# Turning the cross-attention weights on VectorE and regrouping them through DRAM, in a one-core decoder kernel

## The chip, the cores and the metric

The kernel runs on one core of a Trainium2 chip. The metric is the device time of one execution in microseconds (us). Before the change it was 3282.67 us, the median of three runs (3279.49, 3282.67 and 3287.01).

## What is computed

A post-norm decoder layer over 32 sequences of 256 tokens with 256 channels, all in float32. Three sub-layers follow each other, each added to its input and layer-normalised:

```python
# 1. latent self-attention: 16 heads, latent width 72, causal
Wdkv = x @ latent_w + latent_b
q = einsum('btc,hcl->bhtl', x, Wd_w) + Wd_b
attn = softmax(where(causal, q . Wdkv / 4, -inf));  y = attn . Wdkv;  x1 = norm(x + y @ out_w + out_b)
# 2. cross-attention to 120 context rows: 16 heads of width 64
q, k, v = x1 . Wq, ctx . Wk, ctx . Wv
weights = softmax(q k^T / 8);  x2 = norm(x1 + (weights . v) . Wo)
# 3. 16 experts, each of which takes its best 32 tokens of every sequence, and a shared expert
x3 = norm(x2 + routed(x2) + shared(x2))
```

The change concerns the middle sub-layer: `weights` come out of the softmax with the 256 queries on partitions (two tiles of 128) and the 120 keys along the row. The product `weights . v` contracts over the keys, so the weights must first be brought to a layout with the keys on partitions.

## The kernel before

One core does the sequences in **rounds**. In round n (`first_half(n)`, L939, then `second_half(n)`, L1008) TensorE works at three sequences at once: the self-attention of sequence n, the first half of the cross-attention (heads 0 to 7, called c0 = 0) of sequence n-1, and the rest of the cross-attention (heads 8 to 15, c0 = 4) of sequence n-2, with the norm and the store of sequence n-3. The rounds n = 1 to 30 and a first half for n = 31 run under a manual schedule of TensorE (PE), ScalarE (ACT), VectorE (DVE) and GpSimd (POOL): on these four the instructions stand in the order of the calls. The order on SyncE (SP), which issues the DMAs, is left to a scheduler. A tail of calls (`last_scores`, `last_weights`, and the end of the program) finishes the last sequences between the first pieces of the experts, which come after all rounds.

The self-attention of one sequence has four groups of heads. For group g: `queries(n, g)` makes the queries, `scores(n, g)` (L443) the scores, which DVE moves to `sm` while it adds a mask (L474); `peak` (L481) finds the negated maxima on DVE, `ex` (L488) takes exponentials on ACT with their sums, `over` (L497) inverts the sums on DVE and multiplies on POOL, and `turn` (L526) turns `sm` by 32x32 blocks with one DVE instruction (`nc.vector.transpose`, in the profile STREAM_TRANSPOSE, L533). `weigh(n, half)` (L549) multiplies the turned blocks by the values, and SP brings its result `z` to `zT` by DMA, in part through DRAM (`rest`, L581 to L587). `latent_out` (L592) multiplies `zT` by the output weights (36 matmuls), adds x (L602) and takes `moments` (L155): statistics on DVE and one power on POOL (L167). `norm_x1` (L605) normalises, `turn_x1` (L610) transposes x1 on TensorE (four transposes, `px1T`) and copies it to SBUF on DVE (L195). From this `x1T` come the cross queries `pqx` (L658).

The cross-attention of one sequence has four units, (c0, t) with c0 = 0 or 4 (eight heads each) and t = 0 or 1 (128 queries each). For each unit `cross_scores` (L677) makes two PSUM tiles of four heads ("even" and "odd" heads); `cross_peak`, `cross_ex` and `cross_over` do the softmax into a tile `xsm`, 128 queries by four heads by 120 keys, one for the even and one for the odd heads. Then `cross_turn` (L718) does, for each of the two tiles, four TensorE transposes into one PSUM bank and one copy to SBUF: DVE copies the even heads (L733), ACT the odd (L731). When both t of a half are there, `cross_weigh` (L735) multiplies `xpt` by the values. `cross_out` (L757) applies Wo, adds x1 (L767) and takes moments; `norm_x2` normalises, `store_x2` writes rows to DRAM, `turn_x2` transposes on TensorE (`px2T`).

The PSUM banks of all these share a ring of six (`r`); only `cross_scores` has banks of its own.

`keys(n+1)` (L363) makes the latent keys of the next sequence: four matmul instructions (`pk`), a copy with bias on ACT (`kT`, L372) and one on DVE (`kD`, L373). `place_keys` (L375) then sends parts of `kT` to the fixed tile `kr` with four small DMAs, one for each group of heads; each may go only when `scores` of the round before no longer needs that group.

In the order of the calls, `both(cross_turn, ...)` (L892: even, then odd) stands at four places of each round: after `ex(n, 0, 0)` in the first half (unit (0, 1) of sequence n-2), after `turn_x1` (unit (4, 0) of n-2), after `ex(n, 2, 0)` in the second half (unit (4, 1) of n-2) and after `ex(n, 3, 0)` (unit (0, 0) of n-1).

Of the kernel before, what the change touches and what calls it, by code (L numbers as in the profile page):

```python
# [20 lines left out]
F32 = mybir.dt.float32  # L21
# [5 lines left out]
P = 128  # L27
# [5 lines left out]
def decoder_kernel(  # L33
# [213 lines left out]

    vals = wp.tile([P, RB, TC, L], F32, name="vals")
    nc.gpsimd.memset(gw_sb, 0.0)

    raw = ow_sb.rearrange("p a b -> p (a b)").rearrange("p (c n) -> p c n", c=DC)
    by_head = raw.rearrange("p c (h l) -> p c h l", l=L)
# [339 lines left out]
    def latent_out(s):  # L592
        st = states[s]
        po = bank("r", [P, TC, C], f"po_{st['nm']}")
        for t in range(TC):
            project(
                po[:, t, :],
                [(st["zT"][:, c, t * P : (t + 1) * P], ow_sb[:, c, :]) for c in range(ZC)],
            )
        r1 = ap.tile([P, TC, C], F32, tag="r", bufs=1, name=f"r1_{st['nm']}")  # L600
        with urgent():
            nc.vector.tensor_tensor(r1, po, st["x"], ALU.add)  # L602
        st["r1"] = r1, *moments(ap, r1, f"1_{st['nm']}")

    def norm_x1(s):  # L605
        st = states[s]
        st["x1"] = ap.tile([P, TC, C], F32, tag="x1", name=f"x1_{st['nm']}")
        normalised(st["x1"], *st["r1"])

    def turn_x1(s):  # L610
        st = states[s]
# [46 lines left out]
    def cross_queries(s, c0, c):  # L658

        st = states[s]  # L660
        if c == 0:
            st["qxT", c0] = ap.tile([P, HG, T], F32, tag="qxT", name=f"qxT_{st['nm']}_{c0}")
        pqx = bank("r", [P, 2, T], f"pqx_{st['nm']}_{c0 + c}")
        for a in range(2):
            w0 = (c0 + c + a) * P
            project(
                pqx[:, a, :],
                [(wq_sb[:, d, w0 : w0 + P], st["x1T"][:, d, :]) for d in range(DC)],
            )
        dst = st["qxT", c0][:, c : c + 2, :]  # L670
        with urgent():
            if c:
                nc.vector.tensor_scalar(dst, pqx, XSCALE, None, ALU.mult)
            else:
                nc.scalar.mul(dst, pqx, XSCALE)

    def cross_scores(s, c0, t):  # L677
        st = states[s]
# [21 lines left out]
    def cross_ex(s, c0, t, odd):  # L700

        st = states[s]
        nm = f"x{st['nm']}_{c0}_{t}_{odd}"
        sm = ap.tile([P, HG, S2], F32, tag="xsm", bufs=4, name=f"xsm_{nm}")
        st["xrs", odd] = exponentials(sm, st["pL", c0, t][odd], st["xmax", odd], nm)
        st["xsm", c0, t, odd] = sm

    def cross_over(s, c0, t, odd):
        st = states[s]
        divide(st["xsm", c0, t, odd], st["xrs", odd])  # L710

    def cross_weights(s, c0, t):
        cross_peak(s, c0, t)
        for odd in range(2):
            cross_ex(s, c0, t, odd)
            cross_over(s, c0, t, odd)

    def cross_turn(s, c0, t, odd):  # L718
        st = states[s]
        nm = f"{st['nm']}_{c0}_{t}_{odd}"  # L720
        if t == 0:
            st["xpt", c0, odd] = ap.tile(
                [S2, HG, T], F32, tag=f"xpt{odd}", bufs=1, name=f"xpt_{nm}"
            )
        pT = bank("r", [S2, HG, P], f"pxT_{nm}")
        for j in range(HG):
            nc.tensor.transpose(pT[:, j, :], st["xsm", c0, t, odd][:, j, :], ident)  # L727
        dst = st["xpt", c0, odd][:, :, t * P : (t + 1) * P]
        with urgent():
            if odd:  # L730
                nc.scalar.copy(dst, pT)  # L731
            else:
                nc.vector.tensor_copy(dst, pT)  # L733

    def cross_weigh(s, c0):  # L735
        st = states[s]
        if c0 == 0:
            st["cxT"] = ap.tile([P, QC, T], F32, tag="cxT", bufs=1, name=f"cxT_{st['nm']}")
        for j0 in range(0, HG, 2):
            pc = bank("r", [P, 2, T], f"pc_{st['nm']}_{c0}_{j0}")  # L740
            for a in range(2):
                for odd in range(2):
                    nc.tensor.matmul(  # L743
                        pc[odd * DH : (odd + 1) * DH, a, :],
                        st["vx"][:, 2 * (c0 + j0 + a) + odd, :],
                        st["xpt", c0, odd][:, j0 + a, :],
                        start=True,
                        stop=True,
                    )
            dst = st["cxT"][:, c0 + j0 : c0 + j0 + 2, :]  # L750
            with urgent():
                if j0:
                    nc.scalar.copy(dst, pc)
                else:
                    nc.vector.tensor_copy(dst, pc)

    def cross_out(s):  # L757
        st = states[s]
        po2 = bank("r", [P, TC, C], f"po2_{st['nm']}")
        for t in range(TC):  # L760
            project(
                po2[:, t, :],
                [(st["cxT"][:, c, t * P : (t + 1) * P], wo_sb[:, c, :]) for c in range(QC)],
            )
# [3 lines left out]
        st["r2"] = r2, *moments(ap, r2, f"2_{st['nm']}")  # L768

    def norm_x2(s):  # L770
        st = states[s]
        st["x2"] = ap.tile([P, TC, C], F32, tag="x2", bufs=1, name=f"x2_{st['nm']}")
        normalised(st["x2"], *st["r2"])

    def store_x2(s):
        st = states[s]
# [162 lines left out]
    def first_half(n):  # L939
        odd = n % 2 and n > 1  # L940
        run(load, n + 1)
        scores(n, 0)
        run(cross_scores, n - 2, 4, 0)
        run(norm_x2, n - 3)
        run(store_x2, n - 3)
        run(cross_values, n - 1, 0)
        peak(n, 0)
        if n == 1:
            queries(1, 1)
        ex(n, 0, 0)  # L950
        both(cross_turn, n - 2, 0, 1)
        run(cross_peak, n - 2, 4, 0)
        if n != 1:
            queries(n, 1)
        over(n, 0, 0)
        if odd:
            run(cross_values, n - 1, 1)
        run(turn_x2, n - 3)
        ex(n, 0, 1)
        if odd:  # L960
            cross_keys(n // 2, 0, (0,))
        over(n, 0, 1)
        run(cross_ex, n - 2, 4, 0, 0)
        run(cross_over, n - 2, 4, 0, 0)
        weigh(n - 1, 1)
        place_values(n)
        if routed(n):
            route((n - 3) // BQ)
        turn(n, 0, 0)
        run(cross_weigh, n - 2, 0)  # L970
        run(cross_ex, n - 2, 4, 0, 1)
        run(cross_over, n - 2, 4, 0, 1)
        best_of(n, 0)

# [92 lines left out]
    def last_scores():  # L1067
# [1 line left out]
        scores(last, 2)  # L1069
        cross_scores(last - 1, 0, 0)  # L1070
        cross_queries(last - 1, 4, 0)
        both(cross_turn, last - 2, 4, 1)
        weights(last, 2)
        cross_queries(last - 1, 4, 2)
        cross_keys(last // 2, 1)
# [13 lines left out]
    def last_weights():  # L1089

        fill(1)
        turns(last, 3)
        finish_cross(last - 2)
        cross_scores(last - 1, 4, 0)
        both(cross_turn, last - 1, 0, 1)
        cross_weights(last - 1, 4, 0)
        fill(1)
        weigh(last, 1)
        cross_weigh(last - 1, 0)
        turn_x2(last - 2)  # L1100
        latent_out(last)
        norm_x1(last)

    def finish_cross(s):
        cross_out(s)
        norm_x2(s)
        store_x2(s)

# [327 lines left out]
```

## Time and profile before

| | |
|---|---|
| time of the profiled execution | 3281.89 us |
| its span, first to last instruction | 3280.1 us |
| granted TensorE clock, mean of the span | 0.997 |
| busy in the steady rounds (130 to 2150 us of the span): PE, DVE, ACT, POOL | 2004.42, 1343.54, 1105.96, 655.30 of 2020 us |
| share of the DMA engines there, and rate | 0.19, 46 GB/s |
| chain that ended last: PE, DVE | 91%, 5% of the span |
| cross transposes (`pxT`, L727): count, busy | 1024, 134.1 us |

The page of the profile sums each engine's busy time. Its groups give, for each line, engine and shape, the count, the busy time, the mean length of one instruction in ns, and the idle time before it with what ended it. The chain that ended last is followed back from the end, at each step to what released it; read in order of time, it says which engine set the pace at each moment. The timeline gives start and length of each instruction.

TensorE's instructions are pipelined: one can begin before the one before it has ended, so that a length is not the time by which an instruction moves the next. The starts of the next groups are.

### The profile page before, as it was taken

Reading aid. Unit: us, or ns where it says so; the run is one execution under the profiler, and the core shown is the slowest. Engines: PE = TensorE matmul, PEld = TensorE weight load, DVE = VectorE, ACT = ScalarE, POOL = GpSimd, SP = SyncE. Lnnn points to the kernel's source line nnn. Section 1 sums busy time; section 2 is a strip of 40 time slices with the busy share of each in tenths; the row PEclk is TensorE's granted clock in tenths of the full one; section 3 lists DMA queues with packets and bytes.
Section 4 is the critical chain, followed back from the end, with each engine's and each line's share of the span. In section 5 each row is a group of like instructions: output and inputs, shape, how many; then the busy total and the mean of one; then the engine's idle time right before and its main releaser. Section 6 shows DMA issues by size and latency. Waiting matters only on the chain.

```text
span 3280.1 us, 58501 instructions
## 1 busy us (share of the span) xinstructions
PE 3234.2 (99%) x21996; PEld 2375.4 (72%) x21996; DVE 1739.6 (53%) x3576; ACT 1391.5 (42%) x5237; POOL 1069.7 (33%) x951
## 2 busy tenths in 40 slices
PE   8999999999999999999999999999999999999999
PEld 6787778778777877877777878776556656655655
DVE  5666666666666666766666666653312233221133
ACT  4555555555555555555555555544211111111111
POOL 3323332333323323333333233332444302444400
PEclk9999999999999999999999999999999999999999
DMA  4121211111211112112121121133555522555421
GB/s 134 35 48 47 53 46 41 46 47 49 53 42 41 48 47 53 45 38 52 43 57 46 39 49 40 47 80 85 131 123 125 137 76 61 126 124 123 110 77 45
DMA packets 216610, 222.41 MB, mean 68 GB/s; under 512 B 37641, under 2 KB 192265, under 8 KB 216329
## 3 DMA queue, kind: packets, MB, share of 16 engines
q1 hardware_dynamic: 191536, 184.05, 21.0%
q0 software_dynamic: 24576, 34.62, 5.9%
q8 instruction: 175, 2.87, 0.4%
q14 instruction: 107, 0.87, 0.1%
q10 hardware_dynamic: 216, 0.01, 0.0%
HBM read 123.43 MB, written 57.41 MB: 55 GB/s over the span
## 4 chain that ended last, share of the span: by engine, by line
PE 91%; DVE 5%; POOL 1%; ACT 1%; DMA 1%; issue 1%; SPq 0%; POOLq 0%; ACTq 0%
PE po L201 13%; PE pz L559 8%; PE pqx L201 7%; PE pd L201 7%; PE pg L201 7%; PE pu L201 7%; PE pq L201 6%; PE pS L465 5%; PE pc L743 3%; PE pu_s L201 3%; PE pg_s L201 3%; PE pxT L727 3%; PE pfo L201 3%; PE pL L684 3%; PE pS L453 3%; PE pvx L201 3%
## 5 line engine op out<-in xcount | busy, mean ns | idle before, releaser
L499 POOL TENSOR_TENSOR sm<-sm,rs 128x512 f32<-128x512 f32 (+1 forms) x256 | 375.7, 1468 | 1126.1 <-DVE rs L498 1126.0
L488 ACT ACTIVATE sm<-sm,nmax 128x128 f32<-128x128 f32 (+1 forms) x1024 | 451.2, 444 | 105.3 <-DVE nmax L481 105.2
L488 ACT ACTIVATE xsm_x<-pL,nmax_x 128x120 f32<-128x120 f32 x1024 | 351.5, 364 | 3.5 <-DVE nmax_x L481 3.5
L499 POOL TENSOR_TENSOR xsm_x<-xsm_x,rs_x 128x480 f32<-128x480 f32 x256 | 252.7, 987 | 267.2 <-DVE rs_x L498 146.6
L1210 POOL DMA_INDIRECT acc<-eo,offs x128 | 200.8, 1569 | 335.9 <-DVE eo L1207 294.8
L201 PE MATMUL pq<-xT,wd_sb 128*128 128x256 f32 x1152 | 278.7, 382 | 0.3 <-DVE wd_sb L307 0.3
L559 PE MATMUL pz<-d,vals 32*72 32x256 f32 x4608 | 268.4, 380 | 3.7 <-DVE sm L474 1.8
L474 DVE TENSOR_TENSOR sm<-pS,mask 128x384 f32<-128x384 f32 x512 | 247.4, 543 | 36.0 <-PE pS L465 35.9
L201 PE MATMUL po<-ow_sb,zT 128*128 128x256 f32 x1152 | 260.9, 383 | 4.4 <-DMA zT<-z 4.4
L1281 DVE TENSOR_TENSOR hT<-gl,pu 128x512 f32<-128x512 f32 x128 | 87.9, 687 | 333.4 <-PE pu L201 254.2
L533 DVE STREAM_TRANSPOSE d<-sm 128x512 f32<-128x512 f32 (+1 forms) x256 | 244.9, 957 | 23.9 <-POOL sm L499 23.8
L201 PE MATMUL pg<-xeT,wg 128*128 128x512 f32 x512 | 242.3, 596 | 2.3 <-issue 2.3
L201 PEld LDWEIGHTS po<-ow_sb,zT 128*128 128x128 f32 x1152 | 214.3, 190 | 41.7 <-issue 10.0
L201 PE MATMUL pqx<-x1T,wq_sb 128*128 128x256 f32 x1024 | 242.1, 385 | 0.8 <-DVE x1T L195 0.8
L201 PE MATMUL pu<-xeT,wu 128*128 128x512 f32 x512 | 240.7, 592 | 0.0
L559 PEld LDWEIGHTS pz<-d,vals 32*72 32x72 f32 x4608 | 180.4, 139 | 81.9 <-issue 19.1
L481 DVE TENSOR_REDUCE nmax<-sm 128x4 f32<-128x512 f32 (+1 forms) x256 | 231.6, 946 | 3.3
L201 PEld LDWEIGHTS pq<-xT,wd_sb 128*128 128x128 f32 x1152 | 209.0, 190 | 28.1 <-DVE wd_sb L307 0.8
L201 PE MATMUL po<-wo_sb,cxT 128*128 128x256 f32 x1024 | 227.6, 380 | 0.0
L201 PE MATMUL pd<-wd,hT 128*128 128x256 f32 x1024 | 226.6, 379 | 0.0
L488 ACT ACTIVATION_READ_ACCUMULATOR xsm_x<-pL,nmax_x 128x1 f32 x1024 | 216.7, 212 | 0.0
L201 PEld LDWEIGHTS pd<-wd,hT 128*128 128x128 f32 x1024 | 192.1, 190 | 25.7 <-issue 1.0
(135 smaller groups left out, 5513.2 us busy)
## 6 DMA issues: line engine op xcount, KB each, us to landing
zT<-z SPq DMA_DIRECT2D x128, 256.0 KB
wg<-in_wg_dram SPq DMA_DIRECT2D x32, 512.0 KB
wu<-in_wu_dram SPq DMA_DIRECT2D x32, 512.0 KB
wd<-in_wd_dram SPq DMA_DIRECT2D x32, 512.0 KB
vals<-vd SPq DMA_DIRECT2D x128, 72.0 KB
x<-in_x_dram SPq DMA_DIRECT2D x32, 256.0 KB
rows<-x SPq DMA_DIRECT2D x32, 256.0 KB
acc<-x SPq DMA_DIRECT2D x32, 256.0 KB
```

Source lines behind the costliest of these rows:

```text
L201: nc.tensor.matmul(acc, lhsT, rhs, start=(i == 0), stop=(i == n - 1))
L453: nc.tensor.matmul(pS[j][:, SEG[t]], st["q8"][rows, t * P : (t + 1) * P], kr[rows, g, 0 : (t + 1) * P], start=(t == TC - 1), stop=False,)
L465: nc.tensor.matmul(pS[2 * a + odd][:, SEG[t]], st["qT", g][rows, a, t * P : (t + 1) * P], k[rows, 0 : (t + 1) * P], start=False, stop=(t = ...
L474: nc.vector.tensor_tensor(sm[:, j, :], pS[j], mask, ALU.add)
L481: nc.vector.tensor_reduce(nmax, src, AX.X, ALU.max, negate=True)
L488: nc.scalar.activation(dst[:, a, :], src[:, a, :], AF.Exp, bias=nmax[:, a : a + 1], accum_out=rs[:, a, :],)
L499: nc.gpsimd.tensor_tensor(dst, dst, rs.to_broadcast(list(dst.shape)), ALU.mult)
L533: nc.vector.transpose(st["d", t][:, :, k * HG : (k + 1) * HG, :].rearrange("p b h i -> p h b i"), st["sm", g][:, :, SEG[t]].rearrange("p h ...
L559: nc.tensor.matmul(pzs[r][:, t, :], vals[rows, at[0], at[1], :], st["d", t][rows, b].rearrange("p h i -> p (h i)"), start=(i == 0), stop=( ...
L684: nc.tensor.matmul(pLs[odd][:, j, :], st["qxT", c0][rows, j, t * P : (t + 1) * P], pairs[s // 2]["kxT", c0][rows, j, s % 2, :], start=True ...
L727: nc.tensor.transpose(pT[:, j, :], st["xsm", c0, t, odd][:, j, :], ident)
L1210: nc.gpsimd.indirect_dma_start(out=acc[b], out_offset=self.rows(b), in_=eo[:, k, :], in_offset=None, compute_op=ALU.add,)
```

## The change

In the rounds, the weights are no longer turned by TensorE. `cross_spread` turns each `xsm` by 32x32 blocks on DVE, into a tile `xb` that holds both the even and the odd heads. A block turn leaves the four groups of 32 keys side by side in the row and the four groups of 32 queries on partitions; it takes five DMAs from SP to exchange them: `xb` is written to DRAM (512 KB, 4 KB a partition), and four reads, one for each group of 32 keys, bring it back into `xpt` (128 KB each, in runs of 1 KB). `xsm` becomes four fixed tiles, widened to 128 keys, the last eight zero. `xpt` becomes one tile for even and odd heads in which a head's 256 queries lie in eight runs of 32; `cross_weigh` reads them so. `cross_turn` stays for the 16 tiles of the tail.

Beside that, calls move: each `cross_spread` stands later than the `cross_turn` that it takes the place of; the call of `keys(n+1)` moves from the second half to the place before `turn_x1` in the first; the moments are called on their own, those of x2 behind the mask additions of the next `scores`; `norm_x2`, `store_x2` and `turn_x2` stand later; `place_values` stands later; and ACT takes over the second `pqx` copy of each half from DVE.

```diff
+    xsms = [[cw.tile([P, HG, P], F32, name=f"xsm_{o}_{k}") for k in range(2)] for o in range(2)]
...
+            nc.gpsimd.memset(xsms[o][k][:, :, S2:], 0.0)
...
-        st["r1"] = r1, *moments(ap, r1, f"1_{st['nm']}")
+        st["r1"] = r1
+
+    def moments_x1(s):
+        st = states[s]
+        st["m1"] = moments(ap, st["r1"], f"1_{st['nm']}")
...
-            if c:
-                nc.vector.tensor_scalar(dst, pqx, XSCALE, None, ALU.mult)
-            else:
-                nc.scalar.mul(dst, pqx, XSCALE)
+            nc.scalar.mul(st["qxT", c0][:, c : c + 2, :], pqx, XSCALE)
...
+    def by_keys(s, c0, t):
+        st = states[s]
+        if ("xpt", c0) not in st:
+            st["xpt", c0] = ap.tile(
+                [P, TC * RB, 2 * HG, KB], F32, tag="xpt", bufs=1, name=f"xpt_{st['nm']}_{c0}"
+            )
+        return st["xpt", c0][:, t * RB : (t + 1) * RB, :, :]
...
+    def cross_spread(s, c0, t, odd):
+
+        st = states[s]
+        nm = f"{st['nm']}_{c0}_{t}"
+        if odd == 0:
+            st["xb"] = ap.tile([P, RB, 2 * HG, KB], F32, tag="xblk", bufs=1, name=f"xb_{nm}")
+        nc.vector.transpose(
+            st["xb"][:, :, odd * HG : (odd + 1) * HG, :].rearrange("p b h i -> p h b i"),
+            st["xsm", c0, t, odd].rearrange("p h (b i) -> p h b i", i=KB),
+        )
+        if odd == 0:
+            return
+        n = 2 * HG * KB
+        blocks_of = dram.tile([P, RB * n], F32, tag="xblk", bufs=4, name=f"xd_{nm}")
+        nc.sync.dma_start(out=blocks_of, in_=st["xb"].rearrange("p b h i -> p (b h i)"))
+        by_block = blocks_of.rearrange("(r i) (b n) -> b i r n", i=KB, b=RB)
+        dst = by_keys(s, c0, t).rearrange("p r h i -> p r (h i)")
+        for b in range(RB):
+            nc.sync.dma_start(out=dst[b * KB : (b + 1) * KB], in_=by_block[b])
...
-                        st["xpt", c0, odd][:, j0 + a, :],
+                        st["xpt", c0][0:S2, :, odd * HG + j0 + a, :],
...
-        run(norm_x2, n - 3)
-        run(store_x2, n - 3)
+        run(moments_x2, n - 3)
         run(cross_values, n - 1, 0)
         peak(n, 0)
...
+        run(norm_x2, n - 3)
+        run(store_x2, n - 3)
         ex(n, 0, 0)
-        both(cross_turn, n - 2, 0, 1)
...
-        run(turn_x2, n - 3)
         ex(n, 0, 1)
...
         over(n, 0, 1)
+        run(turn_x2, n - 3)
...
-        place_values(n)
...
         run(cross_scores, n - 2, 4, 1)
+        place_values(n)
...
         turn(n, 1, 0)
+        both(cross_spread, n - 2, 4, 0)
         run(cross_over, n - 2, 4, 1, 0)
         latent_out(n - 1)
+        moments_x1(n - 1)
...
         norm_x1(n - 1)
+        run(keys, n + 1)
         turn_x1(n - 1)
-        both(cross_turn, n - 2, 4, 0)
...
         cross_queries(n - 1, 0, 0)
+        both(cross_spread, n - 2, 4, 1)
         cross_queries(n - 1, 0, 2)
...
-        both(cross_turn, n - 2, 4, 1)
         cross_peak(n - 1, 0, 0)
...
-        run(keys, n + 1)
         ex(n, 3, 0)
-        both(cross_turn, n - 1, 0, 0)
         run(place_keys, n + 1)
+        both(cross_spread, n - 1, 0, 0)
         cross_peak(n - 1, 0, 1)
...
         cross_over(n - 1, 0, 1, 1)
+        both(cross_spread, n - 1, 0, 1)
         run(cross_out, n - 2)
```

More of the change, by code (lines that the diff above doesn't have):

```diff
@@ L249, in decoder_kernel @@
     nc.gpsimd.memset(gw_sb, 0.0)
+    xsms = [[cw.tile([P, HG, P], F32, name=f"xsm_{o}_{k}") for k in range(2)] for o in range(2)]
+    for o in range(2):
+        for k in range(2):
+            nc.gpsimd.memset(xsms[o][k][:, :, S2:], 0.0)
     raw = ow_sb.rearrange("p a b -> p (a b)").rearrange("p (c n) -> p c n", c=DC)
@@ L607, in norm_x1 @@
         st["x1"] = ap.tile([P, TC, C], F32, tag="x1", name=f"x1_{st['nm']}")
-        normalised(st["x1"], *st["r1"])
+        normalised(st["x1"], st["r1"], *st["m1"])
     def turn_x1(s):
@@ L669, in cross_queries @@
             )
-        dst = st["qxT", c0][:, c : c + 2, :]
         with urgent():
-            if c:
-                nc.vector.tensor_scalar(dst, pqx, XSCALE, None, ALU.mult)
-            else:
-                nc.scalar.mul(dst, pqx, XSCALE)
+            nc.scalar.mul(st["qxT", c0][:, c : c + 2, :], pqx, XSCALE)
     def cross_scores(s, c0, t):
@@ L703, in cross_ex @@
         nm = f"x{st['nm']}_{c0}_{t}_{odd}"
-        sm = ap.tile([P, HG, S2], F32, tag="xsm", bufs=4, name=f"xsm_{nm}")
-        st["xrs", odd] = exponentials(sm, st["pL", c0, t][odd], st["xmax", odd], nm)
+        sm = xsms[odd][t]
+        st["xrs", odd] = exponentials(sm[:, :, 0:S2], st["pL", c0, t][odd], st["xmax", odd], nm)
         st["xsm", c0, t, odd] = sm
@@ L709, in cross_over @@
         st = states[s]
-        divide(st["xsm", c0, t, odd], st["xrs", odd])
+        divide(st["xsm", c0, t, odd][:, :, 0:S2], st["xrs", odd])
     def cross_weights(s, c0, t):
@@ L720, in cross_turn @@
         nm = f"{st['nm']}_{c0}_{t}_{odd}"
[L721 to L724, printed above, removed]
+        dst = by_keys(s, c0, t)[0:S2, :, odd * HG : (odd + 1) * HG, :]
         pT = bank("r", [S2, HG, P], f"pxT_{nm}")
         for j in range(HG):
-            nc.tensor.transpose(pT[:, j, :], st["xsm", c0, t, odd][:, j, :], ident)
-        dst = st["xpt", c0, odd][:, :, t * P : (t + 1) * P]
+            nc.tensor.transpose(pT[:, j, :], st["xsm", c0, t, odd][:, j, 0:S2], ident)
+        src = pT.rearrange("p h (r i) -> p r h i", i=KB)
         with urgent():
             if odd:
-                nc.scalar.copy(dst, pT)
+                nc.scalar.copy(dst, src)
             else:
-                nc.vector.tensor_copy(dst, pT)
+                nc.vector.tensor_copy(dst, src)
+    def cross_spread(s, c0, t, odd):
[16 more added lines that the diff above has]
+            nc.sync.dma_start(out=dst[b * KB : (b + 1) * KB], in_=by_block[b])
     def cross_weigh(s, c0):
@@ L767, in cross_out, with moments_x2 @@
             nc.vector.tensor_tensor(r2, po2, st["x1"], ALU.add)
-        st["r2"] = r2, *moments(ap, r2, f"2_{st['nm']}")
+        st["r2"] = r2
+    def moments_x2(s):
+        st = states[s]
+        st["m2"] = moments(ap, st["r2"], f"2_{st['nm']}")
     def norm_x2(s):
@@ L772, in norm_x2 @@
         st["x2"] = ap.tile([P, TC, C], F32, tag="x2", bufs=1, name=f"x2_{st['nm']}")
-        normalised(st["x2"], *st["r2"])
+        normalised(st["x2"], st["r2"], *st["m2"])
     def store_x2(s):
@@ L1071, in last_scores @@
         cross_queries(last - 1, 4, 0)
-        both(cross_turn, last - 2, 4, 1)
         weights(last, 2)
@@ L1101, in last_weights @@
         latent_out(last)
+        moments_x1(last)
         norm_x1(last)
@@ L1105, in finish_cross @@
         cross_out(s)
+        moments_x2(s)
         norm_x2(s)
```

## The prediction, made before the changed kernel had run

> **What bounds the kernel now.** I read the page first (busy time), then the groups by shape, then the chain that ended last in order of time over two rounds (1080 to 1180 us), then the timeline where that chain leaves TensorE.
>
> The page's first line, and three groups (count, then busy us, mean ns of one, idle time before them):
>
> ```profile
> PE 3234.2 (99%) x21996; PEld 2375.4 (72%) x21996; DVE 1739.6 (53%) x3576; ACT 1391.5 (42%) x5237; POOL 1069.7 (33%) x951
> ...
> L727 PE MATMUL pxT<-ident,xsm_x 128*120 128x128 f32 x1024 | 134.1, 274 | 2.2 <-POOL xsm_x L499 2.2
> ...
> L733 DVE COPY xpt<-pxT 120x512 f32<-120x512 f32 x128 | 87.7, 685 | 5.2 <-PE pxT L727 1.3
> L533 DVE STREAM_TRANSPOSE d<-sm 128x512 f32<-128x512 f32 x128 | 87.7, 685 | 3.6 <-POOL sm L499 3.5
> ```
>
> TensorE is busy almost always; DVE has a third of each round free (1343.54 of 2020 us busy), ACT nearly half. So a microsecond taken from TensorE is a microsecond of the kernel until another engine's chain is late. The chain by time (start, us, what) shows what TensorE's pieces are worth and where it is near to waiting:
>
> ```profile
> 1105.67 0.70 DVE r L602
> 1106.39 0.75 DVE st L163 x2
> 1107.66 0.69 POOL rstd L167
> 1108.37 1.80 DVE x L173 x2
> 1110.22 0.55 PE px1T L191 x3
> 1110.77 0.87 PE pxT L727 x8
> 1111.64 3.63 PE pqx L201 x16
> ...
> 1135.90 0.86 PE pk L201 x4
> 1136.76 0.87 PE pxT L727 x8
> 1137.64 0.86 PE pq L201 x4
> ```
>
> Eight transposes (one call for even and odd) hold the chain for 0.87 us. The norm of x1 is on the chain itself, and the eight transposes behind `px1T` are what TensorE does while DVE copies `x1T`.
>
> **What goes.** Only 16 of the 256 tiles are still turned by `cross_turn`, so 960 transposes go: 120 calls of eight. By their starts this is 120 x 0.87 = **104.4 us**, 3.48 us in each of 30 rounds. (By the busy column it would be 960 x 134.1 / 1024 = 125.7 us. The Trainium skill, Perfetto Trace Analysis, Identifying the Most-Contended Engine, holds matmul busy time a bad measure because matmuls are pipelined; the trace agrees, 0.109 us from start to start against 0.131 busy; by the busy column the sum below would be 3183.)
>
> **What other engines gain or lose in a round.** DVE: eight block turns of the shape of L533, 8 x 0.685 = 5.48, less four copies L733 (2.74) and two `pqx` copies L673 (2 x 0.691): +1.4 us. ACT: less four copies L731 (4 x 0.572), plus two `pqx` copies (2 x 0.598): -1.1. POOL nothing. No engine becomes the bound by its sum; what counts is the order. The new right operand of `cross_weigh` and the copies into it lie in runs of 32; DVE's copy of `z`, into runs of 32 too, takes 681 ns for 512 columns against 685 for L733, so I cost this at nothing. TensorE's price for it no row shows: nothing, or at worst twice the present 1.88 us of a `pc` piece.
>
> **Wait 1: x1T.** The cover of the `x1T` copy goes, and `pk` stands before `px1T`. Two rows give the order of the copies of `pk`:
>
> ```profile
> 1136.80 0.47 ACT L372 ACTIVATE kT<-pk,latb 96x256 f32<-96x256 f32 x1
> ...
> 1137.30 0.48 DVE L373 TENSOR_SCALAR kD<-pk,latb 64x256 f32<-64x256 f32 x1 [1.03 <-ACT kT L372]
> ```
>
> ACT first, then DVE; and `kD` now stands on DVE before the copy of `x1T`. In the round of 1105 us: TensorE ends its other work at 1109.55, `pk` at 1110.41 (before the norm would hold it up no more), `kT` from 1110.61 to 1111.08, `kD` to 1111.59, `x1T` (0.69) to 1112.28, `pqx` 1112.33 instead of 1111.64: 0.7 us later though eight transposes are gone, and `pk` (0.86) is gone from the second half. Net -0.16 instead of -0.87: 0.7 lost. In the next round `pkx` ends at 1178.66, so `pk` at 1179.52, `kT` 1180.19, `kD` 1180.70, `x1T` 1181.39, `pqx` 1181.44 instead of 1180.96: net -0.38 instead of -0.87, 0.5 lost. Mean 0.6 x 30 = **18 us lost**. Behind `kD` on DVE wait `x1T`, a turn and the new block turns, all due later. `kT` earlier frees `place_keys` to go earlier; its four DMAs stand on SP among the new reads, each behind the `scores` that reads its part, and have the better part of a round.
>
> **Wait 2: x2T.** At the end of a round DVE has, in order: the last turn of `sm`, the last reciprocal, two block turns, the addition r2, four mask additions (1.94), the moments (1.17), two maxima (1.80), the norm of x2 (0.72). In the round that starts at 1063.68 with `scores(n, 3)`, call this 0: the last reciprocal was at 14.36 and comes 0.85 earlier, since ACT has lost `kT` and a copy ahead of it; 0.3 later POOL starts its product (0.99), and the second block turn (0.69) waits for that and ends at 15.6. Then 15.6 + 0.73 + 1.94 + 1.17 + 1.80 + 0.72 = 22.0 for x2. TensorE comes to `px2T` at 24.16 - 0.86 (`pk`) - 2 x 0.87 = 21.5. So in rounds of even n it waits some 0.6 us; in those of odd n it has 3.3 us more to do here (another `pvx`, `pkx`) and less before it, and doesn't wait. 15 x 0.6 = **9 us lost**. The moments moved behind the mask additions keep these from being later still.
>
> **The DMA trip.** The last block turn ends at 15.6; `cross_weigh` needs the data after `weigh`, at 26.7 (even) or 27.9 (odd). No row has this trip; near to it are SP's issues and the wait in the chain:
>
> ```profile
> 1163.28 0.27 SPq L581 DMA_DIRECT2D rest<-z  x1
> 1163.61 1.33 SPq L583 DMA_DIRECT2D zT<-z  x2
> ...
> 1166.08 0.49 SPq L587 DMA_DIRECT2D zT<-rest  x1
> ```
>
> ```profile
> 1163.61 0.65 SPq L583
> 1164.31 4.31 DMA zT<-z
> 1168.76 6.30 PE po L201 x28
> ```
>
> 64 KB had landed in DRAM 2.8 us after the start of their issue; two of 256 KB in runs of 1 KB 5.0 us after theirs. So the write of 512 KB takes 2.8 to 5.0. The reads are issued one after the other (0.66 each, as L398: 1.99 for three) and the last lands 2.8 to 5.0 after its issue: 2.0 + 2.8 to 2.0 + 5.0. Sum 7.6 to 12.0; I take 5.0 + 2.0 + 2.8 + 0.2 for SP = **10.0**, by `zT` for the write (same size) and by `rest` for the small last read. Landing at 25.6, 1.1 before it is due in even rounds and 2.3 in odd ones: nothing lost; with the upper end 0.9 x 15 = 14 us. The other group (c0 = 4) is due some 3 us later in its trip than this one. On SP the reads wait for their write and hold up what stands behind: for this group the stores of x2 and the loads of `vals`, which are not due before `weigh` ends, and then `rest`, `zT`, as before. `xb` has one buffer, so a block turn also waits for the write of the one before it, issued 7 us earlier. `xsm` is fixed now, so an exponential waits for a block turn of the same tile half a round before. `place_values` moves in the calls, but on SP its loads keep their places, three before `rest` and one after: nothing.
>
> **Sum.** 3281.9 (profiled execution; the median of the runs is 0.8 above) - 104.4 + 18 + 9 = **3205**.
>
> **Rivals.**
> (a) *The trip through DRAM is late.* Place: the first `cross_weigh` of each round; it waits T - 11.1 (even) or T - 12.3 (odd). For: five issues in line on one queue, a write that must land before the reads go, 0.2 of the DMA engines in use already. Against: the rows above, which end at 12.0. The forecast's gain of 77 us is 2.6 a round, so this decides from T = 14.3; at T = 16 it costs 4.3 x 30 = 129 us: 3334. (The Trainium skill, VectorE: DVE Perf Modes, The three transpose paths, warns that a plain DMA copy that transposes by strides is 19 times slower than the crossbar when the innermost destination stride is large, and its Rules for kernel authors leave a 128x128 transpose to TensorE. Here DVE has turned inside the blocks and the DMA moves runs of 1 KB; `zT<-z`, in runs of 1 KB, shows no such factor. By that rule the trip would be far beyond 14.3; beyond (a) I give it no chance of its own.)
> (b) *Nothing is late.* POOL and DVE run ahead of my sums, `kD` doesn't wait: 3281.9 - 104.4 = 3177.5. Against: the same order of `kT` and `kD` in both rounds looked at.
> (c) *DVE's chains are later than I sum them*, by up to a microsecond in each of the two waits and in odd rounds too, since the order is fixed and gaps between engines add up: 2 x 30 = 60 us more, 3265. For: DVE has 1.4 us more in a round that gets shorter. Against: a third of DVE's time is free.
> That the transposes stay on TensorE is excluded: the order of the changed program has 240 block turns for them.
>
> **Chances.** Forecast, within 20 us: 0.52. (b): 0.10. (c) and what lies between it and the forecast: 0.14. Within 0.2% (6.6 us, about what a measurement tells from no change): 0.05, a trip of some 14 us. Slower, by (a) or by a slow right operand (30 x 3.8 = 113 us): 0.19. So faster 0.76, same 0.05, slower 0.19. The range goes from (b) to a trip of about 14.5 us: 3178 to 3288; I leave out 0.05 below and 0.13 above.
>
> **What would show it.** Right: `pxT` L727 left with 64 instructions; idle time of `pqx` before DVE `x1T` near 18 us and of `px2T` before DVE x2 near 9; `pc` with no idle time before DMA `xpt`; steady rounds some 2.6 us shorter. Wrong: `pc` waiting for DMA (a), `pc` pieces longer than 1.88 us, or DVE's r2 and mask additions ending idle time on TensorE in odd rounds (c). The forecast fails if SP holds the last write back behind another wait.

## The result, and the profile after

The changed kernel takes **3211.17 us** (median of four runs, 3210.65 to 3212.54), against 3284.84 us for the kernel before on the same chip (four runs, 3279.49 to 3288.32): a ratio of 0.978, with an interval of 0.976 to 0.980. Its profiled execution took 3211.46 us with a span of 3209.7 us and a mean granted clock of 0.997, as before. That is 70.4 us less than the profiled execution of before (3281.89 us), 2.3 us in each of 30 rounds.

The page of the changed kernel begins with the busy times:

```profile
PE 3129.1 (97%) x21036; PEld 2276.3 (71%) x21036; DVE 1754.4 (55%) x3632; ACT 1360.9 (42%) x5181; POOL 1071.3 (33%) x955
```

TensorE's busy time fell by 3234.2 - 3129.1 = 105.1 us. Its idle time (span less busy) rose from 3280.1 - 3234.2 = 45.9 to 3209.7 - 3129.1 = 80.6 us, by 34.7. 105.1 - 34.7 = 70.4, the whole difference: by this split 105 us of work went, and a third of it came back as waiting. The split is not sharp, as the waits below show. DVE has gained 14.8 us, ACT has lost 30.6.

The groups by shape of the same kernel (count, busy us, mean ns, idle time before them and its releasers):

```profile
L201 PE MATMUL pqx<-x1T,wq_sb 128*128 128x256 f32 x1024 | 237.8, 385 | 38.0 <-DVE x1T L195 38.0
...
L753 DVE STREAM_TRANSPOSE xb<-xsm 128x512 f32<-128x512 f32 x240 | 156.3, 680 | 17.0 <-POOL xsm L504 17.0
L775 PE MATMUL pc<-xpt,vx 120*64 120x256 f32 x1024 | 124.6, 385 | 0.0
...
L739 PE MATMUL pxT<-ident,xsm 128*120 128x128 f32 x64 | 9.0, 278 | 2.4 <-POOL xsm L504 2.4
```

64 transposes are left; the 240 block turns cost 680 ns each; and `pc`, whose right operand now lies in runs of 32, has no idle time before it at all. The new idle time stands in front of `pqx`. TensorE's waits (in all us, how often, longest), of before and then of after:

```profile
PE px1T L191 <- DVE x L173: 13.2, 45, 0.6
PE po L201 <- DMA zT<-z: 4.4, 8, 1.6
```

```profile
PE pqx L201 <- DVE x1T L195: 38.0, 31, 1.4
PE po L201 <- DMA zT<-z: 6.7, 12, 1.6
PE px2T L191 <- DVE x L173: 4.6, 3, 1.5
...
PE px1T L191 <- DVE x L173: 1.3, 3, 0.6
```

The wait for x1 moved, from `px1T` to `pqx`, and grew: +37.2 (`pqx` waited 0.8 before) and -11.9 make 25.3 us of the 34.7. Part of a wait can also count as busy time. The groups of `px1T`, before and then after, have the same 128 transposes:

```profile
L191 PE MATMUL px1T<-ident,x 128*128 128x128 f32 x128 | 27.0, 295 | 14.2 <-DVE x L173 13.2
```

```profile
L191 PE MATMUL px1T<-ident,x 128*128 128x128 f32 x128 | 20.7, 280 | 1.4 <-DVE x L173 1.3
```

Before, the first transpose of a round ran ahead and the other three waited for the second half of x1: in the round of 1105 us they started 0.64 us after it (1109.58 and 1110.22), of which the list has 0.34 as idle. So 6.3 us of the 105.1 are this wait, and with them the net loss at x1 is 19.0 us rather than 25.3. The chain that ended last, in order of time (start, us, what), shows one such place:

```profile
1012.56 0.88 PE pk L201 x4
...
1013.46 0.48 ACT kT L377
...
1013.97 0.48 DVE kD L378
...
1014.48 0.70 DVE x1T L195
...
1015.22 3.72 PE pqx L201 x16
```

From the end of `pk` to `pqx` three copies follow one another for 1.78 us. Of these TensorE covers 0.5 with `px1T`; 1.23 us a time is idle (38.0 / 31).

The trip through DRAM, on the timeline of the round of 1049 us (DVE's last block turn, SP's write, SP's four reads, and the product that needs them):

```profile
1049.79 0.71 DVE L753 STREAM_TRANSPOSE xb<-xsm 128x512 f32<-128x512 f32 x1 [0.57 <-POOL xsm L504]
1050.53 0.34 SPq L761 DMA_DIRECT2D xd<-xb  x1
1053.13 1.73 SPq L765 DMA_DIRECT2D xpt<-xd  x4
...
1061.60 1.95 PE L775 MATMUL pc<-xpt,vx 120*64 120x256 f32 x16
```

and the table by stretches over it (us, PE busy, PEld, DVE, ACT, POOL, granted clock, share of the DMA engines, GB/s):

```profile
1054.90:1056.30 1.40, 1.40 (x8) 1.25 (x7) 1.40 (x3) 1.22 (x5) 0.54 (x1) 1.00 0.78 251
1056.30:1057.50 1.20, 1.14 (x7) 0.52 (x5) 1.20 (x5) 1.20 (x8) 0.00 (x0) 1.00 0.04 10
```

The reads go 2.6 us after the write, and by 1056.3 or soon after the DMA engines are idle: the trip lasts some 5.9 us from the end of the block turn (1050.50). It is due 11.1 us after it (1061.60). In the next round block turn and product are 12.4 us apart (1115.48 and 1127.88).

### The profile page after: what moved, and what is told of

Its sections match the earlier page's. It is cut to its first block, busy times and chain, and to the rows that moved or that the text cites. A ratio compares the mean times of both kernels' runs of the same rounds, so it can differ in the third digit from the quotient of the medians.

```text
span 3209.7 us, 57226 instructions
## 1 busy us (share of the span) xinstructions
PE 3129.1 (97%) x21036; PEld 2276.3 (71%) x21036; DVE 1754.4 (55%) x3632; ACT 1360.9 (42%) x5181; POOL 1071.3 (33%) x955
## 4 chain that ended last, share of the span: by engine, by line
PE 86%; DVE 5%; DMA 3%; ACT 3%; issue 1%; POOL 1%; SPq 1%; POOLq 0%; ACTq 0%; DVEq 0%
PE po L201 11%; PE pz L564 8%; PE pqx L201 7%; PE pd L201 7%; PE pu L201 7%; PE pg L201 7%; PE pq L201 7%; PE pS L470 5%; PE pu_s L201 3%; PE pg_s L201 3%; PE pfo L201 3%; PE pc L775 3%; PE pvx L201 3%; PE pL L689 3%; PE pkx L201 3%; PE pS L458 3%
## 5 line engine op out<-in xcount | busy, mean ns | idle before, releaser
L493 ACT ACTIVATE xsm<-pL,nmax_x 128x120 f32<-128x120 f32 x1024 | 351.7, 365 | 2.2 <-DVE nmax_x L486 2.2
L504 POOL TENSOR_TENSOR xsm<-xsm,rs_x 128x480 f32<-128x480 f32 x256 | 252.7, 988 | 240.9 <-DVE rs_x L503 239.9
L201 PEld LDWEIGHTS po<-ow_sb,zT 128*128 128x128 f32 x1152 | 214.3, 190 | 44.5 <-issue 12.4
L201 PEld LDWEIGHTS pq<-xT,wd_sb 128*128 128x128 f32 x1152 | 214.1, 190 | 43.7 <-issue 11.1
L201 PEld LDWEIGHTS pqx<-x1T,wq_sb 128*128 128x128 f32 x1024 | 189.4, 190 | 72.6 <-DVE x1T L195 45.4
L167 POOL TENSOR_TENSOR rstd<-rstd,mhalf 128x2 f32<-128x2 f32 (+1 forms) x97 | 67.3, 693 | 507.3 <-DVE rstd L166 455.7
```

The costliest lines, as they stand in the source:

```text
L201: nc.tensor.matmul(acc, lhsT, rhs, start=(i == 0), stop=(i == n - 1))
L493: nc.scalar.activation(dst[:, a, :], src[:, a, :], AF.Exp, bias=nmax[:, a : a + 1], accum_out=rs[:, a, :],)
L504: nc.gpsimd.tensor_tensor(dst, dst, rs.to_broadcast(list(dst.shape)), ALU.mult)
```

## The experiments

Theory: the 35 us that came back are the copies `kT`, `kD`, `x1T` in line before `pqx` (25), x2 a little late, and `zT`; the DMA trip costs nothing, since it is hidden with 5 us to spare. Rivals: the moved calls themselves do harm or good apart from that line; the loss is the extra DMA traffic; or the trip is nearer to its due time than it looks. In the table, idle is TensorE's span less its busy time.

| kernel | median us | ratio to before, interval | idle us |
|---|---|---|---|
| the change | 3211.17 | 0.978, 0.976 to 0.980 | 80.6 |
| keys_behind_turn | 3196.87 | 0.974, 0.972 to 0.975 | 60.9 |
| kD_behind_x1T | 3193.95 | 0.973, 0.972 to 0.974 | 66.0 |
| keys_as_before | 3219.16 | 0.981, 0.979 to 0.982 | 79.3 |
| moves_alone | 3280.69 | 0.999, 0.998 to 1.000 | 53.6 |
| block_turns_alone | 3212.71 | 0.978, 0.977 to 0.980 | 73.9 |
| one_more_hop | 3232.60 | 0.984, 0.983 to 0.986 | 103.4 |
| two_more_hops | 3622.84 | 1.103, 1.100 to 1.106 | 366.5 |
| two_hops_first_half_only | 3425.72 | 1.043, 1.040 to 1.046 | 236.3 |
| cover_q8 | 3181.52 | 0.968, 0.967 to 0.969 | 49.5 |
| cover_q8_early_x2 | 3177.26 | 0.967, 0.966 to 0.969 | 47.9 |

**kD behind the copy of x1T.**

```diff
-            nc.vector.tensor_scalar(st["kD"][LM:], pk[0:LM], latb[0:LM], None, ALU.add)
+        st["pk"] = pk
...
+    def keys_odd(s):
+        st = states[s]
+        with urgent():
+            nc.vector.tensor_scalar(st["kD"][LM:], st.pop("pk")[0:LM], latb[0:LM], None, ALU.add)
...
         turn_x1(n - 1)
+        run(keys_odd, n + 1)
```

> The changed kernel with only the DVE copy kD moved behind the copy of x1T; pk stays ahead of px1T on TensorE and kT stays on ACT. Theory (kD, waiting for kT, holds the x1T copy): the copy starts some 0.55 us sooner, 16 us in all: 3195; idle time of pqx before x1T falls from 38.0 to about 21, since nothing covers the copy itself (0.69 us). Rival (the copy waits for px1T or the norm, not for kD): no change, 3211.

It took 3193.95 us, 17 less than the change. Its waits and its chain:

```profile
PE pqx L201 <- DVE x1T L195: 22.8, 31, 0.8
```

```profile
1069.10 0.45 PE px1T L191 x4
1069.57 0.70 DVE x1T L195
1070.32 3.72 PE pqx L201 x16
```

`kD` (0.48 us and its step) is out of the line, and the wait fell by 15.2 us, 0.49 each time. What is left is the copy of `x1T` itself, 0.74 us from the end of `px1T` to `pqx`, which the eight transposes covered before.

**keys behind turn_x1.** `pk` itself then stands between `px1T` and `pqx`, as the eight transposes did.

```diff
-        run(keys, n + 1)
         turn_x1(n - 1)
+        run(keys, n + 1)
```

> The changed kernel with keys(n+1) called just behind turn_x1 instead of just ahead of it, so that TensorE's four pk instructions (0.86 us) stand between px1T and pqx, and kD stands behind the x1T copy on DVE. Theory (TensorE sets the pace and loses its time at the x1T copy, which waits for kT on ACT and kD on DVE): pk covers the copy as the transposes did, pqx comes 0.69 us sooner in even and 0.48 in odd rounds, about 18 us in all: 3193; idle time of pqx before DVE x1T falls from 38.0 to under 8, that of px1T before the norm rises from 1.3 to about 13. Rival (the wait only moves to the norm of x1, whose chain of DVE and POOL sets the pace here): no change, 3211.

It took 3196.87 us. Its waits:

```profile
PE px1T L191 <- DVE x L173: 14.8, 45, 0.8
PE po L201 <- DMA zT<-z: 9.5, 12, 1.9
PE px2T L191 <- DVE x L173: 4.6, 3, 1.5
```

The wait of `pqx` is down to the 0.8 us of before, and that of `px1T` is back. Two ways of breaking the same line gain 14 and 17 us: the line `kT`, `kD`, `x1T` is shown to cost that much.

**keys as before.** The call goes back to the second half, between `peak(n, 3)` and `ex(n, 3, 0)`.

> The changed kernel with keys(n+1) back in the second half, ahead of ex(n, 3, 0), where it stood before the change. Theory: nothing stands between px1T and pqx, but x1T no longer waits for kD, while px1T waits for the norm again; 0.1 us slower in even, 0.4 in odd rounds: 3218, within 3212 to 3226. Rival (that place of the keys is what keeps the gain of the eight transposes there): 0.86 us a round slower, 3237.

It took 3219.16 us, 8 more than the change:

```profile
PE pqx L201 <- DVE x1T L195: 22.8, 31, 0.8
PE px1T L191 <- DVE x L173: 13.1, 45, 0.6
```

Both waits stand side by side now, 35.9 us against 39.3 in the change. By the list alone it would be 3 us faster; but busy time is 9.0 us longer (3138.1 against 3129.1), 6.3 of it in `px1T`, which is split by its wait again (27.0 us against 20.7). So moving `keys` is a little better than leaving it, but it is its place against `turn_x1` that counts: one line further down it is worth 22 us, not 8.

**The moves alone, and the block turns alone.** In the first, `cross_turn` stays at its four places and all moved calls stay moved. The second is the kernel before with `cross_spread` at the places of the change, and no other call moved.

```diff
-        both(cross_spread, n - 2, 4, 0)
...
+        both(cross_turn, n - 2, 4, 0)
```

> The changed kernel with its weights turned by TensorE again: cross_turn at its four old places, no block turns and no DMAs for them; all the moved calls (keys, moments, norm_x2, store_x2, turn_x2, place_values, the pqx copy on ACT) stay. Theory (the gain is TensorE's time for 960 transposes; the moves only decide what is waited for): near the kernel before, 0.2 to 0.4 us a round off for pk as a cover: 3276, within 3268 to 3284. Rival (a good part of the gain comes from the moves, through DVE, which loses two copies a half): 3260 or below.

> The kernel before with the block turns and their DMAs at the places where the change has them, and with none of the other moves: keys, moments, norm_x2, store_x2, turn_x2, place_values and the pqx copies as before. Theory: the gain stays but for the x1T copy, which nothing covers now and which then also waits for the norm: near the version with the keys as before, 3214, within 3206 to 3224; idle time of px2T gone, since x2 no longer waits behind the mask additions and maxima. Rival (the moves are needed, since DVE's chain at the end of a round with moments ahead of the mask additions stops TensorE): 3240 or above.

The moves alone took 3280.69 us (ten runs) against 3284.07 (15 runs): 3 us. The block turns alone took 3212.71, the same as the whole change. Their waits, first of the moves, then of the block turns:

```profile
PE pqx L201 <- DVE x1T L195: 15.8, 30, 1.4
```

```profile
PE pqx L201 <- DVE x1T L195: 22.8, 31, 0.8
PE px1T L191 <- DVE x L173: 14.6, 45, 0.8
PE po L201 <- DMA zT<-z: 4.0, 7, 1.6
```

Even with the eight transposes as a cover, `kD` in the line makes `pqx` wait 15.8 us. Neither kernel has a wait of `px2T` for x2 in the list: the 4.6 us of the change need the block turns and the moved moments and norm together. The moves take away the wait of `px1T` and add as much elsewhere; the gain of the change is that of the block turns. These two runs also price the transposes like for like: with the moves on both sides TensorE's busy time fell by 3229.3 - 3129.1 = 100.2 us, without them by 3234.2 - 3136.2 = 98.0. And the wait of `po` for `zT`, 4.4 us before and 6.7 in the change, is 8.4 with the moves and none of the new DMAs, and 4.0 with the new DMAs and no moves.

**One more hop.** Each block is copied once more inside DRAM before it is read.

```diff
         nc.sync.dma_start(out=blocks_of, in_=st["xb"].rearrange("p b h i -> p (b h i)"))
+        for hop in range(1):
+            again = dram.tile([P, RB * n], F32, tag=f"xhop{hop}", bufs=4, name=f"xh{hop}_{nm}")
+            nc.sync.dma_start(out=again, in_=blocks_of)
+            blocks_of = again
```

> The changed kernel with one more copy of each 512 KB block from DRAM to DRAM between the write and the four reads, so that the trip gets about 2.8 us longer; the output is the same. Theory (the trip takes some 6 us of 11 to 13, by the trace of the changed kernel, and is hidden): at most a few us slower, 3211 to 3220. Rival (the trip is what TensorE's first cross_weigh of a round comes near to waiting for): 2.8 us x 30 = 84 us slower, 3295.

It took 3232.6 us, 21 more than the change: outside what either side had said. The timeline of an even round, whose last block turn ended at 1063.85 (write, hop, reads, product):

```profile
1063.88 0.36 SPq L761 DMA_DIRECT2D xd<-xb  x1
1067.22 0.49 SPq L764 DMA_DIRECT2D xh<-xd  x1
...
1070.96 1.78 SPq L769 DMA_DIRECT2D xpt<-xh  x4
...
1076.49 1.95 PE L779 MATMUL pc<-xpt,vx 120*64 120x256 f32 x16 [1.46 <-ACT z L582]
```

The product starts 12.6 us after the block turn and has waited 1.46, so it was due at 11.2. (The releaser named is not the real one, as can be when several semaphores are waited for: in the change the product at 1061.60 starts before ACT's copies of z, at 1061.73, so it does not need them.) The next, odd round does not wait. Over the whole run:

```profile
L779 PE MATMUL pc<-xpt,vx 120*64 120x256 f32 x1024 | 127.4, 391 | 24.4 <-DMA acc<-x 7.8 <-DMA xpt<-xh 7.1 <-DMA vals<-vd 5.5
```

The waits are uneven: 11 even rounds have 16.4 us of them (one alone 5.5), 5 odd ones 5.5 (one alone 3.2), and one product of heads 8 to 15 has 1.7. Most products don't wait at all. So the trip is near its due time with one hop, and how late it comes varies from round to round; what was wrong in the expectation was the length of the hop. The copy itself took 3.7 us; the write before it 3.3 instead of 2.6, and the reads after it were slower to land too (5.5 from the first issue to the product, where 3.3 were enough in the change): 6.7 in all in this round where I had put 2.8.

**Two more hops.** `range(2)` in place of `range(1)`.

> The changed kernel with two more copies of each 512 KB block from DRAM to DRAM between its write and its reads. From the run with one more hop: the trip was 5.9 us without a hop and about 12.4 us with one, and there an even round lost what went beyond 11.1 us, an odd round nothing up to 12.4. A second copy of about 3.7 us makes the trip about 16 us. If the price of a late trip is its length past 11.1 us in an even and past 12.3 us in an odd round, TensorE loses 4.9 and 3.7 us, 4.3 us on average over 30 rounds, about 129 us over the changed kernel: about 3340 us (3310 to 3360), and the wait of the cross product pc for DMA grows from about 20 to 110 to 130 us, now in nearly every round, odd ones too. Rival: what the one hop cost was not lateness of the trip but the displaced issues on the sync engine's queue, a fixed sum for each hop: then a second hop adds another 21 us, about 3254 us, with pc's wait near 40 us.

It took 3622.84 us, 283 above the forecast and far beyond the rival. The group of `pc`:

```profile
L779 PE MATMUL pc<-xpt,vx 120*64 120x256 f32 x1024 | 219.4, 602 | 292.6 <-DMA xpt<-xh 254.8 <-DMA rest<-z 32.2 <-DMA zT<-z 5.6
```

Against the change, idle time rose by 366.5 - 80.6 = 286 us and busy time by 3255.1 - 3129.1 = 126 us. Two things had been left out. First, there are 59 waits, not 30: the product of heads 8 to 15 was late too. Its last write stands on SP behind the reads of the trip before, and goes some 3 us after its block turn (at 1125.71, the turn ended at 1122.81; the product followed at 1141.32, 18.5 us after the turn; in the round before 3.25 us). Second, a `pc` matmul took 602 ns on the mean instead of 385. The timeline shows when (the last bracket is the wait):

```profile
1062.09 1.95 PE L779 MATMUL pc<-xpt,vx 120*64 120x256 f32 x16 [2.88 <-DMA xpt<-xh]
...
1079.43 0.33 SPq L761 DMA_DIRECT2D xd<-xb  x1
...
1082.68 0.47 SPq L764 DMA_DIRECT2D xh<-xd  x1
...
1087.26 1.67 SPq L764 DMA_DIRECT2D xh<-xh  x1
...
1092.03 1.75 SPq L769 DMA_DIRECT2D xpt<-xh  x4
...
1096.58 3.68 PE L779 MATMUL pc<-xpt,vx 120*64 120x256 f32 x16 [5.01 <-DMA xpt<-xh]
```

After this wait of 2.88 us the 16 matmuls take 1.95 us as ever; after the one of 5.01 they take 3.68, and so do most groups of this kernel (634 ns a matmul, against 379). The granted clock shows why. In the wait of 5.01 it is 1.00 in the stretch from 1093.38 and 0.50 in that from 1094.98, still in the wait. Around another wait, of 2.21 us before 1220.25 (third number from the end: the clock):

```profile
1219.45:1220.25 0.80, 0.00 (x1) 0.03 (x1) 0.61 (x2) 0.00 (x0) 0.64 (x1) 1.00 0.06 17
1221.85:1222.65 0.80, 0.80 (x7) 0.35 (x3) 0.80 (x2) 0.00 (x0) 0.00 (x0) 0.50 0.98 201
1225.05:1225.85 0.80, 0.80 (x14) 0.73 (x12) 0.28 (x1) 0.00 (x0) 0.00 (x0) 1.00 0.00 0
```

The clock falls to 0.50 during a long wait, or soon after a shorter one, and is back some microseconds later; over stretches of 500 us in the rounds its mean is 0.92 to 0.94, against 0.99 to 1.00 in the change. The Trainium skill, TensorE: Matmul & The Clock Gate, Part 1: The HAM clock gate, has this as a rule: about one idle window of 3.4 us puts the clock to half, and some 3.4 us of work bring it back. The trace agrees on the half clock, but shows no sharp limit: every wait of `pc` of 3.4 us or more was followed by slow matmuls, at least in part; of the shorter ones 2.88 us left the product at 1.95 us, while 2.21, 2.31, 2.95 and 2.99 were followed by 2.90, 2.91, 3.63 and 3.61.

**Two more hops for the first half of the heads only**, to test that reading: `range(0 if c0 else 2)`.

> Two extra copies from DRAM to DRAM only in the trips of heads 0 to 7 (c0 = 0); the trips of heads 8 to 15 (c0 = 4) as in the changed kernel. With two copies in every trip the kernel took 3622.8 us, far over the 3340 expected, and its trace gives two reasons: both cross products of a round waited for DMA (292.6 us in 59 waits, 5.0 each), and after nearly all of those waits the 16 matmuls of pc took 634 ns each instead of 379, a piece of 3.68 instead of 1.95 us, with all of TensorE's busy time 126 us up. If a late trip costs what each product waits, plus a slow piece behind each wait above some 3 to 4 us, then with only the c0 = 0 trips late: 30 waits of 5.0 (even rounds) and 4.2 (odd) make 138 us, 30 slow pieces make 52 us, other slow matmuls some 10: about 200 us over the changed kernel, 3410 us (3385 to 3435), with about 30 slow pc groups of 64 and none among those of c0 = 4. Rival: the excess came from the crowding of the sync engine's one queue by all the copies together, and with half of them gone the c0 = 0 trips are shorter: then no more than the 107 us worked out from the prediction's price for the first product (4.3 us less a fifth, 30 times) plus nothing for the clock, 3320 to 3340 us.

It took 3425.72 us; 3410 was expected (3385 to 3435), 3320 to 3340 by the rival. The group, and a product of either kind:

```profile
L779 PE MATMUL pc<-xpt,vx 120*64 120x256 f32 x1024 | 171.2, 492 | 161.2 <-DMA xpt<-xh 138.8 <-DMA rest<-z 22.4
```

```profile
1130.24 1.95 PE L779 MATMUL pc<-xpt,vx 120*64 120x256 f32 x16
...
1166.09 3.68 PE L779 MATMUL pc<-xpt,vx 120*64 120x256 f32 x16 [7.37 <-DMA xpt<-xh]
```

30 waits of 5.4 us are 161 us (138 were expected), and TensorE's busy time rose by 3187.8 - 3129.1 = 59 us, 47 of it in `pc` (62 and 52 expected). The groups of c0 = 4, as the one at 1130.24, neither wait nor slow down. Crowding of SP's queue by the copies is not the main cause, then. The price of a late trip is the wait plus the slow clock behind it.

**Cover for the copy of x1T.** With `kD` out of the line, 22.8 us of `pqx` were left. The third `pq` piece of the next sequence (`query_rest`), which nothing needs so early, is put where the eight transposes stood.

```diff
         turn_x1(n - 1)
         run(keys_odd, n + 1)
+        run(query_rest, n + 1)
...
-        run(query_rest, n + 1)
```

> The version with kD behind x1T, and query_rest(n+1), 0.86 us of TensorE, moved from the second half to the place just behind turn_x1, as a cover for the x1T copy. Theory: idle time of pqx before x1T falls from 22.8 to under 4, worth 20 us; TensorE then comes 0.86 us sooner to px2T in even rounds, where x2 is late already, which gives back up to 13 us: 3181, within 3172 to 3190; px2T's wait for x2 rises from 4.6 to 10 or more. Rival (TensorE is no longer what sets the pace, DVE is): 3192 or more.

3181.52 us, as expected; `pqx` is down to 0.8 us, as before the change, and the wait of `px2T` rose by less than expected (6.0, not 10 or more). The longest waits for x2 and `zT`:

```profile
PE po L201 <- DMA zT<-z: 10.1, 13, 2.1
PE px2T L191 <- DVE x L173: 6.0, 3, 2.0
```

**The same, with x2 as early as before.** The moments of x2 are called inside `cross_out` again, and `norm_x2` and `store_x2` stand ahead of the maxima.

> The version before with the moments of x2 back with the addition r2, ahead of the mask additions, and the norm of x2 ahead of the maxima, as before the change. Theory: x2 is there 1.8 us sooner, px2T doesn't wait, and the later mask additions cost nothing: 3172, within 3166 to 3180. Rival (the mask additions set the pace, which is why the moments were put behind them): slower than the version before, 3185 or more.

3177.26 us, 34 below the change: the fastest kernel here. `px2T` waits 1.0 us in all, and one wait is longer than before:

```profile
PE po L201 <- DMA zT<-z: 14.4, 18, 1.7
```

The gain over cover_q8 is 4 us by medians, with runs that overlap (3174.84 to 3179.01 against 3173.65 to 3185.18); that the wait went is plain, that the time did is not settled. Idle time is 47.9 us now, 2.0 above the kernel before, with 105.3 us of busy time gone. All the new DMAs are still there, so they alone did not bring the 35 us back.

## Why the prediction was right, point by point

The forecast was 3205 us; 3211 was measured, inside its range and its main case.

- *What goes, 104.4 us.* 105.1 went from TensorE's busy time. That it comes so near is partly luck: 6.3 of it are the shorter `px1T`, and like for like the transposes took 98.0 and 100.2. The working by starts was right to some 6 us; the 125.7 of the busy column would have been 20 us or more off.
- *Other engines.* ACT -30.6 us (-33 forecast), POOL +1.6. DVE gained 14.8 instead of 1.4 x 30 = 42: oversized, without effect on the time.
- *The strided right operand at nothing.* Right: 124.6 us and 385 ns for `pc` in both kernels.
- *Wait 1, 18 us.* The mechanism was right (`kT`, then `kD`, then `x1T`), and kD_behind_x1T and keys_behind_turn show it. The size is 25.3 net by the list of waits, 19.0 with the shorter busy time of `px1T`. The working put `pqx` 1.92 us behind the end of `pk`, 1.37 of it idle, 41 us in 30 rounds; 38.0 were measured. From this it took back 23 for the wait of `px1T` that goes, from two rounds with 0.7 and 0.9 us; the list of waits of before has 13.2 us, and 6.3 more were hidden in busy time, 19.5 in all. So this term was nearly right, and the 7 us by which the gain was too high (77 forecast, 70.4 in the profiled executions) are spread: a few in what goes, a few in small waits such as that for `zT`. The split into busy and idle is too blurred to say how many lie where. The sign "idle time of `pqx` near 18" was worded wrongly with it: 18 was the net loss, and the idle time would have been 41 by the same working.
- *Wait 2, 9 us.* The list of waits has 4.6, in three places 533 us apart, 1.52 each, not in every even round. In the even round of 1049 us x2 ended at 1057.02 and the four transposes began at 1056.84 without idle time, 0.78 long instead of 0.60: late by 0.2, not 0.6. In every even round the four took 0.78, in every odd one 0.60, so even rounds alone are late, as forecast; the group of `px2T` is 2.5 us longer in all (21.8 against 19.3). With the 4.6 this makes 7.1 of the 9. In the place read, at 791 us, DVE does eight conversions for the experts (L913, 1.01 us at 784.89) between r2 and the mask additions, which the working did not have.
- *The trip, 10.0 us.* It took 5.9, below the lower bound of 7.6. The write took 2.6 (5.0 taken), the reads 3.3 (4.8 taken). The due times, 11.1 and 12.3, were right to 0.1. Hidden, as forecast.
- *Rival (a).* Its place was right, and mostly in even rounds. one_more_hop cost 21 us, and for the 12.6 us of the trip that was read the formula gives 1.5 x 15 = 22; but the waits were not alike, so the match is partly luck. Its price beyond that was too low. With one half of the heads late, the two trips read from the trace took 16.8 and 18.5 us; by the formula 17.65 - 11.7 = 5.95 us a round, 178 in all, near the 161 of waiting that were measured, but 59 of slower matmuls come on top, which the formula lacks. With all trips late the second product of a round waits as well. The prediction left it out for its later due time, but 12.2 and 15.7 us of room (block turns ended at 1044.71 and 1114.56, products at 1056.95 and 1130.24 in the last of these runs) don't hold a trip of 18.
- *Rival (b), nothing late, 3177.5.* Not the change, but the kernel that it describes: cover_q8_early_x2 took 3177.26. The match is partly luck too: there `po` waits 10.0 us more than before, and `px1T` 11.6 less.
- *Rival (c).* No wait of TensorE for r2 is in the list, and for the masks only one of 1.8 us (`pz`), which before had too.
- *Not forecast.* `po` waited 2.3 us more for `zT`, and in the fastest kernel 10 us more than before. For the change the traffic (111 GB/s in the rounds, 46 before) is not the cause by itself: block_turns_alone has the new DMAs and waits 4.0, moves_alone has none and waits 8.4. For the fastest kernel no run here separates it from everything else coming sooner.

That a transpose of this size belongs on TensorE, as the Trainium skill has it (VectorE: DVE Perf Modes, Rules for kernel authors), does not hold where TensorE is the bound: here two block turns of 0.680 us on DVE and 5.9 us of hidden DMA replaced 0.87 us of TensorE for every eight transposes.

## What to carry to other kernels

When work leaves the engine that is the bound, look at what that work was covering: 35 of 105 us came back here, most of it at one copy that eight transposes used to hide, and a piece of work without an early due time put in the same place brought part of it back (12 us, cover_q8). When a call is moved ahead of a critical copy, follow each of its own copies through the queues of the engines that make them: half a microsecond of `kD` in front of `x1T` cost 17 us, and one line further down it costs nothing. Size a wait over the whole run, and look at the busy time of the groups beside it as well as at the list of waits: of some 19.5 us that `px1T` lost before the change, the list had 13.2.

## What the runs showed of the hardware

A trip of 512 KB from SBUF to DRAM and back, in rows of 4 KB out and runs of 1 KB in, took 5.9 us beside a busy TensorE, at 251 GB/s while the reads landed. A copy of the same block inside DRAM held SP's next issue of the trip back by 3.7 to 4.8 us in most rounds read, and once by 6.2. A right operand in eight runs of 32 floats cost TensorE nothing (385 ns a matmul on the mean, as before). Waits of TensorE cost more than themselves when they are long: after the waits of 3.4 us or more in the runs with two more hops, and after some of 2.2 to 3.2, the matmuls were slow, up to 3.68 us for 16 instead of 1.95, and the granted clock, where it was read, was 0.50 for some microseconds.
